# Two attention layers on one core: the third product bank behind the products with v, and the place of the quarter sums

## The chip, the core and the metric

The kernel runs on one core of one Trainium2 chip. The metric is the device time of one launch in microseconds (us), the median of three runs. The profile is of one further execution, recorded by the hardware profiler.

## What is computed

Two transformer layers in float32 over 4 images of 32 x 32 tokens and 768 channels, 12 heads of 64. Both normalise in groups, make q, k and v, add a relative-position bias to the scores, take the softmax, weigh v, project, and add the result to the input. The second also convolves q, k and v (3 x 3, per channel) and normalises them per head.

```python
# layer 0, of gn(x)
q, k, v = heads(x @ Wq + bq), heads(x @ Wk + bk), heads(x @ Wv + bv)
attn = q @ k.T / sqrt(64) + rel_bias_h[..., :, None] + rel_bias_w[..., None, :]
x = x + (softmax(attn) @ v) @ Wp + bp
# layer 1, of gn(x)
q, k, v = split(x @ w_qkv.T)
q, k, v = (layer_norm(dwconv3x3(t, w_pool)) for t in (q, k, v))
attn = q @ k.T * 64**-0.5 + rel_h[..., :, None] + rel_w[..., None, :]
x = x + (softmax(attn) @ v + q) @ w_proj.T + b_proj
```

## The kernel before

**Stages and pairs.** A stage is one image in one layer; the eight stages run in the order images 0 and 1 in layer 0, images 0 and 1 in layer 1, then images 2 and 3 likewise. A stage has six pairs of heads, so there are 48 pairs, counted from 0: pairs 0 to 5 are stage 0, pairs 12 to 23 and 36 to 47 belong to layer 1. While one pair is attended, the next is prepared. In layer 1 the preparation reaches further: a pair's first products are made half a pair earlier still.

**Steps.** `attend` (L663) goes through a pair in two halves of 512 queries (`c`), each in two batches of four key tiles (`g`). A batch makes four score tiles of 128 keys x 2 heads x 512 queries on TensorE (L724 q with k, L726 the bias), each followed by one exponential on ScalarE (L731) and one addition on VectorE into the running sum `acc` (L738, L740). Then come two steps of other work, behind the scores. Then follow the products with v (L746), and two more steps of other work, behind the products with v. A pair thus has 16 steps: 0, 1, 4, 5, 8, 9, 12, 13 lie behind scores and 2, 3, 6, 7, 10, 11, 14, 15 behind products with v. The sums over keys (z, L688) and the result's operations (L695 to L716) of a half are spread over the windows of the next half through the list `rest`.

**The order is written out by hand.** `plan` (L596) gives each pair's pieces with their steps, `at` (L787) files pieces under a step, and the loop at L827 issues them at that step in the order in which they were filed. Each engine works through its own instructions in that order. The pieces that matter here, with their steps in the pair before the one that they prepare:

- Layer 1: `padded(V, 0)` at 2, `centre(Q)` at 3 (two banks), `positions(0)` at 10, `positions(1)` at 11, `back(K, 0)` and `back(K, 1)` at 14, `split` at 12. Of the pair after that, `padded(Q, 1)` at 10 and `padded(K, 1)` at 14 (its steps -6 and -2).
- Layer 0: `sevens(Q, .)` at 0 and 2, `positions` at 6 and 8, `split` at 10. `sevens` uses a scheme of seven products of quarters in place of eight; its sums of quarters of the activations come from `mix_tokens` (L272), five additions on VectorE of 128 x 1536 elements (L280), two of them in place in `xn`, three into the shared buffer `quarters`.
- `split` (L577) rounds the bias on ScalarE (`high`, L582), subtracts it on VectorE (L583), and issues 16 DMAs on POOL (L593) that lay `high` and the rest, `whole`, out as the bias tiles.
- `group_norm` (L283) of the next stage in twelve pieces; its mean (`gn_mean`, L298, read on VectorE at L300) falls on step 14 of a stage's third pair.
- `project` (L758) of the stage before: twelve products in the first pair of a stage, each read on VectorE (L780). For image 0 in layer 1 a small product, `pbias` (L770), stands ahead of every second one.

**The banks of PSUM.** There are eight. `ps_a` has two, one pair of banks for the first and fourth score tile of a batch. `place_b` and `place_c` have two each, used as a pair by the second and the third score tile, and as single banks by the other work in between. One holds the products with v, and one, the sums' bank (`ps_small`), holds z, the small products of the group norm, `pbias`, and one of the products of `sevens`. Other work asks for a single bank through `bank` (L117), and `other_work` (L113) sets the order of places: behind scores b, b, c, c, behind products with v c, c, b, b, and round again. A tile that takes a place waits until the readers of what was there are done.

**The moved sums.** Where the stage before is of layer 0 too, `mix_tokens` stands on steps 72 to 76, counted from the first step of the stage before (L801); the pieces of that stage's last pair that read the quarters stand on 64 and 66, and the first piece that reads the new ones on 80. This happens for stages 1 and 5, so in pairs 4 and 28.

Of the kernel before, what the change touches and what calls it, by code (L numbers as in the profile page):

```python
# [45 lines left out]
def two_layers(ctx: ExitStack, tc: tile.TileContext, keep, x_in, wqkv, wproj, rels, windows, vrow, small, const, onehot, picks, out):  # L46
# [60 lines left out]

    place_b, place_c = Place("left"), Place("right")  # L110
    places = [place_b, place_c]

    def other_work(first, second):  # L113
        places[:] = [first, second]
        first.n = second.n = 0

    def bank(name):  # L117

        place = places[0]
        ps = place.single(name)  # L120
        if place.n % 2 == 0:
            places.reverse()
        return ps

    def small_bank(name):
        return ps_small.tile([P, 512], F32, tag="small", name=name)
# [20 lines left out]
    def col(c, lo=0, hi=P):  # L147
        return sm[lo:hi, c : c + 1]
# [15 lines left out]
    stages = [(b0 + k, layer) for b0 in range(0, B, 2) for layer in range(2) for k in range(2)]  # L164
# [38 lines left out]
    def shift(i):  # L203

        return 4 if i and items[i][1] == 0 and items[i - 1][1] == 1 else 0
# [3 lines left out]
    for i, (_, layer, hp) in enumerate(items):  # L209
        first = (i - 1) * 16 + shift(i)  # L210
# [8 lines left out]
    def load_xn(stage):  # L219
        b, layer = stage  # L220
        xn = xnp.tile([P, NC, T], F32, tag="xn", name="xn")
        src = rows(mid[b] if layer else x_in[b])
        for n in range(NC):
            nc.sync.dma_start(xn[:, n, :], src[:, n, :])
        xns[stage] = xn
# [46 lines left out]
    def mix_tokens(stage):  # L272


        x11, x12, x21, x22 = (xns[stage][:, n : n + 3, h : h + HALF] for n in (0, 3) for h in (0, HALF))
        for to, x, y, op in (
            (quarters[1], x11, x12, ALU.add), (x12, x12, x22, ALU.subtract), (quarters[2], x21, x22, ALU.add),
            (x21, x21, x11, ALU.subtract), (quarters[0], x11, x22, ALU.add),
        ):
            nc.vector.tensor_tensor(to, x, y, op)  # L280
            yield
# [57 lines left out]
    class Pair:  # L339
# [86 lines left out]
        def product(self, s, h):  # L426
            xn, w = xns[self.b, self.layer], weights[self.i, s]
            ps = bank("qkv")
            for n in range(NC):
                halves(ps, w[:, n, :], xn[:, n, h * HALF : (h + 1) * HALF], n == 0, n == NC - 1)  # L430
            if h:
                used((self.i, s))
            return ps
# [229 lines left out]
    def attend(pair, os):  # L663


        q, k, bias = pair.q, pair.k, pair.bias
        os.append(q)
        nonlocal found
        heads = [slice(j * D, (j + 1) * D) for j in range(2)]

        def more():
            nonlocal found
            if rest:
                found = rest.pop(0)(*found)

        for c in range(T // QC):
            cols = slice(c * QC, (c + 1) * QC)

            def copy(av):
                weighed = one.tile([P, QC], F32, tag="weighed", name="weighed")  # L680
                nc.scalar.copy(weighed, av)  # L681
                return weighed

            def sums(weighed, acc, c=c):

                z = small_bank("z")
                for j in range(2):
                    nc.tensor.matmul(  # L688
                        z[j * D : (j + 1) * D, :], cst[:, ONES : ONES + D], acc[:, j, :],
                        start=True, stop=True,  # L690
                    )
                at = 2 * (pair.i * (T // QC) + c)
                t = work.tile([P, QC], F32, tag="t", name="t", bufs=1)
                inv = work.tile([P, QC], F32, tag="inv", name="inv", bufs=1)
                nc.scalar.activation(t, z, AF.Copy, accum_out=seen[:, at : at + 1])  # L695

                nc.scalar.activation(inv, t, AF.Ln, bias=tiny)
                nc.scalar.activation(inv, inv, AF.Exp, scale=-1.0, accum_out=seen[:, at + 1 : at + 2])
                return weighed, t, inv

            def result(weighed, t, inv, cols=cols):

                nc.vector.scalar_tensor_tensor(t, t, -1.0, inv, ALU.mult, ALU.mult)
                nc.vector.scalar_tensor_tensor(inv, t, 2.0, inv, ALU.add, ALU.mult)

                if pair.layer:
                    nc.vector.tensor_tensor(inv, weighed, inv, ALU.mult)
                    nc.vector.scalar_tensor_tensor(q[:, cols], inv, col(LN + 4), q[:, cols], ALU.mult, ALU.add)
                else:
                    nc.vector.tensor_tensor(inv, weighed, inv, ALU.mult)  # L710
                return (inv,)

            def finish(inv, cols=cols):

                if not pair.layer:
                    nc.scalar.activation(q[:, cols], inv, AF.Identity, bias=col(pair.column(2)))  # L716

            for g in range(0, NKT, 4):
                es = []
                for kt, place in zip(range(g, g + 4), (None, place_b, place_c, None)):  # L720
                    keys = slice(kt * P, (kt + 1) * P)
                    ps = place.pair("s") if place else ps_a.tile([P, 2, 512], F32, tag="a", name="s")
                    for j, rows in enumerate(heads):
                        nc.tensor.matmul(ps[:, j, :], k[rows, keys], q[rows, cols], start=True, stop=False)  # L724
                    for j, rows in enumerate(heads):
                        nc.tensor.matmul(  # L726
                            ps[:, j, :], ones[rows, keys], bias[c][rows, kt // 2, :],
                            start=False, stop=True,
                        )
                    e = work.tile([P, 2, QC], F32, tag="e", name="e", bufs=4)  # L730
                    nc.scalar.activation(e, ps, AF.Exp)  # L731
                    es.append(e)
                other_work(place_b, place_c)
                more()
                if g == 0:
                    av = ps_av.tile([P, QC], F32, tag="av", name="av")
                    acc = work.tile([P, 2, QC], F32, tag="acc", name="acc", bufs=1)
                    nc.vector.tensor_tensor(acc, es[0], es[1], ALU.add)  # L738
                for e in es[2 * (g == 0) :]:
                    nc.vector.tensor_tensor(acc, acc, e, ALU.add)  # L740
                yield
                yield
                for t, e in enumerate(es):
                    kt = g + t
                    for j in range(2):
                        nc.tensor.matmul(  # L746
                            av[j * D : (j + 1) * D, :], pair.vt[:, kt, j * D : (j + 1) * D], e[:, j, :],
                            start=(kt == 0), stop=(kt == NKT - 1),
                        )
                other_work(place_c, place_b)  # L750
                more()
                if g + 4 == NKT:
                    rest.extend((sums, result, finish))
                    found = (copy(av), acc)
                yield
                yield
# [30 lines left out]
    def at(step, piece):  # L787
        events.setdefault(step, []).append(piece)

    n_steps = NKT * (T // QC)  # L790
    oss = [[] for _ in stages]
    for k in range(1, len(stages)):
        first = (k - 1) * NC * n_steps
        at(first + n_steps, lambda k=k: load_xn(stages[k]))
        norm = group_norm(stages[k])
        for r in range(12):
            at(first + 2 * n_steps + 2 + 3 * r, lambda norm=norm: next(norm, None))
        if stages[k][1] == 0:
            mix = mix_tokens(stages[k])
            for r in range(5):  # L800
                at(first + 5 * n_steps + (r // 3 if stages[k - 1][1] else r - 8), lambda mix=mix: next(mix, None))  # L801
        elif stages[k - 1][1] == 0:
            at(first + 4 * n_steps + 6, lambda: [nc.gpsimd.memset(pad, 0.0) for pad in pads])
    mix = mix_tokens(stages[0])
# [11 lines left out]
    for k, stage in enumerate(stages):  # L816
        steps = project(stage, oss[k])
        first = (k + 1) * NC * n_steps
# [7 lines left out]
    step = 0  # L826
    for i, pair in enumerate(pairs):  # L827
        for _ in attend(pair, oss[i // NC]):
            for piece in events.pop(step, ()):
                piece()  # L830
            step += 1
# [311 lines left out]
```

## Time and profile before

| what | us |
|---|---|
| median of three runs (3982.46 to 3984.02) | 3983.66 |
| the profiled execution | 3979.48 |
| its span | 3977.6 |
| TensorE busy | 3898.5 |
| VectorE busy | 2492.3 |
| ScalarE busy | 1840.8 |
| POOL busy | 411.5 |

PE is TensorE's matmul side, PEld its weight loads, DVE VectorE, ACT ScalarE, POOL GpSimd. A line of the timeline has the start and the duration in us, engine, line and operation, then what is written and read (out<-in), how many instructions were merged into it, and in brackets the idle time before it with what ended it. A line of the waits has the waiting instruction, what it waited for, the time in us, how often, and the longest. Idle time of TensorE is what counts, as it is the fullest engine. Its matmuls are pipelined and their ends are modelled, so the distance from one start to the next is the measure.

### The profile page before, as it was taken

The page shows a single profiled execution, that of the slowest core. Times are in us where ns is not written, and L with a number is a line of the kernel's source. Part 1 is how long each engine was busy: PE and PEld are TensorE (multiplying, and loading weights), DVE is VectorE, ACT ScalarE, POOL GpSimd, SP SyncE. Part 2 cuts the span into 40 slices and gives each one's busy share as a digit, 9 for nine tenths or more (in the row PEclk, how much of TensorE's full clock was granted, in tenths as well). Part 3 has the DMA queues.
Part 4 walks back from the last instruction along what each step waited for, and adds up shares of the span by engine and source line. Part 5 has one row for each costly group of instructions (what it writes and reads, how often), then busy time and mean ns, then how long its engine had stood idle before and what let it go on. Part 6 is the DMA issues. An engine that isn't in the chain of part 4 may idle for free.

```text
span 3977.6 us, 79975 instructions
## 1 busy us (share of the span) xinstructions
PE 3898.5 (98%) x35026; PEld 1736.9 (44%) x35026; DVE 2492.3 (63%) x2794; ACT 1840.8 (46%) x2717; POOL 411.5 (10%) x776
## 2 busy tenths in 40 slices
PE   7999999999999999999899999999999999999999
PEld 3535434534344444444444445355443444434443
DVE  2455524557489984799633554245675898848883
ACT  2454424555355552455433544254542555425552
POOL 0111100110000100000011010001100011000010
PEclk9999999999999999999999999999999999999999
DMA  5343242221411312212133222423124121131122
GB/s 161 85 117 115 72 135 74 65 55 50 131 44 34 91 38 86 63 41 70 42 110 89 54 72 64 147 58 76 43 59 124 38 50 47 44 104 42 38 47 76
DMA packets 179044, 293.33 MB, mean 74 GB/s; under 512 B 22528, under 2 KB 77952, under 8 KB 178688
## 3 DMA queue, kind: packets, MB, share of 16 engines
q1 hardware_dynamic: 117248, 187.41, 15.1%
q0 software_dynamic: 61440, 100.71, 11.0%
q8 instruction: 279, 4.57, 0.5%
q14 instruction: 77, 0.63, 0.0%
HBM read 153.36 MB, written 34.01 MB: 47 GB/s over the span
## 4 chain that ended last, share of the span: by engine, by line
PE 90%; DVE 6%; DMA 2%; issue 1%; ACT 1%; POOL 0%; DVEq 0%; SPq 0%; ACTq 0%
PE qkv L131 19%; PE s L724 15%; PE av L746 15%; PE proj L131 13%; PE m3m L131 4%; PE m4m L131 4%; PE s L726 4%; PE m1m L131 4%; PE ln_c L131 3%; PE rel L566 3%; PE z L688 2%; PE m L131 2%; DVE shared L508 2%; DVE acc L740 2%; PE ln_t L544 1%
## 5 line engine op out<-in xcount | busy, mean ns | idle before, releaser
L731 ACT ACTIVATE e<-s 128x1024 f32<-128x1024 f32 x768 | 780.7, 1025 | 470.6 <-PE s L726 437.4
L724 PE MATMUL s<-q,k 64*128 64x512 f32 x3072 | 817.3, 608 | 11.1 <-ACT whole L572 7.6
L740 DVE TENSOR_TENSOR acc<-acc,e 128x1024 f32<-128x1024 f32 x576 | 705.6, 1225 | 184.9 <-ACT e L731 135.5
L131 PE MATMUL qkv<-xn,wqkv_t 128*64 128x512 f32 x3648 | 815.7, 596 | 2.9 <-DVE xn L314 2.9
L508 DVE SCALAR_TENSOR_TENSOR shared<-shared,sm 128x1056 f32<-128x1056 f32 x576 | 758.4, 1317 | 14.9
L726 PE MATMUL s<-bias,ones 64*128 64x512 f32 x1536 | 613.6, 792 | 14.5 <-DMA bias<-whole 9.6
L746 PE MATMUL av<-e,vt 128*64 128x512 f32 x2624 | 594.2, 594 | 0.0
L593 POOL DMA_DIRECT2D bias<-high x384 | 204.0, 549 | 3295.5 <-ACT high L582 3047.3
L131 PE MATMUL proj<-q,wproj_t 128*64 128x512 f32 x2304 | 504.2, 593 | 0.0
L131 PEld LDWEIGHTS qkv<-xn,wqkv_t 128*64 128x64 f32 x3648 | 253.8, 137 | 487.5 <-issue 482.2
L491 ACT ACTIVATE shared<-qkv,sm 128x512 f32<-128x512 f32 (+1 forms) x288 | 129.3, 502 | 591.2 <-PE qkv L131 591.2
L724 PEld LDWEIGHTS s<-q,k 64*128 64x128 f32 x3072 | 277.7, 187 | 281.1 <-issue 203.9
L746 PEld LDWEIGHTS av<-e,vt 128*64 128x64 f32 x2624 | 185.2, 137 | 346.7 <-issue 319.2
L738 DVE TENSOR_TENSOR acc<-e 128x1024 f32<-128x1024 f32 x96 | 117.5, 1224 | 305.0 <-ACT e L731 293.8
L131 PEld LDWEIGHTS proj<-q,wproj_t 128*64 128x64 f32 x2304 | 163.2, 137 | 316.4 <-issue 315.9
L726 PEld LDWEIGHTS s<-bias,ones 64*128 64x128 f32 x1536 | 150.0, 188 | 202.8 <-issue 194.7
L593 POOL DMA_DIRECT2D bias<-whole x384 | 206.0, 563 | 121.5 <-DVE whole L583 112.0
L681 ACT COPY weighed<-av 128x512 f32<-128x512 f32 x96 | 56.4, 587 | 301.7 <-PE av L746 301.7
L780 DVE SCALAR_TENSOR_TENSOR x<-proj,sm,x 128x512 f32<-128x512 f32 x48 | 36.1, 751 | 217.4 <-PE proj L131 213.1
L780 DVE SCALAR_TENSOR_TENSOR x<-proj,pbias,x 128x512 f32<-128x512 f32 x48 | 36.0, 750 | 216.1 <-PE proj L131 211.7
L131 PEld LDWEIGHTS ln_c<-cst,shared 128*64 128x64 f32 x2304 | 131.7, 138 | 48.9 <-issue 41.4
L131 PE MATMUL ln_c<-cst,shared 128*64 128x128 f32 x2304 | 139.7, 275 | 6.9 <-DVE shared L508 6.2
(121 smaller groups left out, 3744.8 us busy)
## 6 DMA issues: line engine op xcount, KB each, us to landing
bias<-high POOLq DMA_DIRECT2D x384, 128.0 KB, 2.8
bias<-whole POOLq DMA_DIRECT2D x384, 128.0 KB, 3.0
wqkv_t<-in_wqkv SPq DMA_DIRECT2D x78, 384.0 KB, 3.1
wqkv_t<-mixed SPq DMA_DIRECT2D x66, 384.0 KB, 3.1
wproj_t<-in_wproj SPq DMA_DIRECT2D x48, 384.0 KB, 3.8
wqkv_t<-in_wqkv SPq DMA_DIRECT2D x66, 192.0 KB, 2.5
xn<-in_x SPq DMA_DIRECT2D x24, 512.0 KB, 7.6
x<-in_x SPq DMA_DIRECT2D x48, 256.0 KB, 2.8
```

What stands on the lines that cost most here:

```text
L131: nc.tensor.matmul(ps[lo : lo + D], a[:, lo : lo + D], b, start=start, stop=stop, **kw)
L491: nc.scalar.activation(self.pad[s][:, rows, there : there + src.shape[2]], src, AF.Identity, bias=col(self.column(s)))
L508: nc.vector.scalar_tensor_tensor(y, window, tap, y, ALU.mult, ALU.add)
L566: nc.tensor.matmul(ps[lo : lo + S, k * S : (k + 1) * S].rearrange("p (b c) -> p b c", b=2), rel[rows, 2 * self.layer + i, first : first + ...
L593: nc.gpsimd.dma_start(sets, some.unsqueeze(1).to_broadcast([D // 2, 2, QC]))
L688: nc.tensor.matmul(z[j * D : (j + 1) * D, :], cst[:, ONES : ONES + D], acc[:, j, :], start=True, stop=True,)
L724: nc.tensor.matmul(ps[:, j, :], k[rows, keys], q[rows, cols], start=True, stop=False)
L726: nc.tensor.matmul(ps[:, j, :], ones[rows, keys], bias[c][rows, kt // 2, :], start=False, stop=True,)
L731: nc.scalar.activation(e, ps, AF.Exp)
L738: nc.vector.tensor_tensor(acc, es[0], es[1], ALU.add)
L740: nc.vector.tensor_tensor(acc, acc, e, ALU.add)
L746: nc.tensor.matmul(av[j * D : (j + 1) * D, :], pair.vt[:, kt, j * D : (j + 1) * D], e[:, j, :], start=(kt == 0), stop=(kt == NKT - 1),)
```

## The change

Behind the products with v, the third request for a single bank in a window gets the sums' bank (`small_bank`) instead of a bank of place_b; the order there becomes c, c, sums' bank, b, b. Behind scores it stays b, b, c, c. And where a stage of layer 0 follows one of layer 0, the five quarter sums of `mix_tokens` are issued on steps 68, 68, 69, 69, 70 instead of 72 to 76.

```diff
     place_b, place_c = Place("left"), Place("right")
-    places = [place_b, place_c]
-
-    def other_work(first, second):
-        places[:] = [first, second]
-        first.n = second.n = 0
+    behind_scores, behind_av = (place_b, place_b, place_c, place_c), (place_c, place_c, None, place_b, place_b)
+    turn = list(behind_av)
+
+    def other_work(places):
+        turn[:] = places
+        place_b.n = place_c.n = 0
 
     def bank(name):
 
-        place = places[0]
-        ps = place.single(name)
-        if place.n % 2 == 0:
-            places.reverse()
-        return ps
+        place = turn.pop(0)
+        turn.append(place)
+        return place.single(name) if place else small_bank(name)
...
-                other_work(place_b, place_c)
+                other_work(behind_scores)
                 more()
...
-                other_work(place_c, place_b)
+                other_work(behind_av)
                 more()
...
             mix = mix_tokens(stages[k])
             for r in range(5):
-                at(first + 5 * n_steps + (r // 3 if stages[k - 1][1] else r - 8), lambda mix=mix: next(mix, None))
+                step = 5 * n_steps + r // 3 if stages[k - 1][1] else 4 * n_steps + 4 + r // 2
+                at(first + step, lambda mix=mix: next(mix, None))
```

## Prediction

> **What bounds the kernel now.** I read the busy times first, then the waits of TensorE, then the timeline around each wait that the change can touch.
>
> ```profile
> PE 3898.5 (98%) x35026; PEld 1736.9 (44%) x35026; DVE 2492.3 (63%) x2794; ACT 1840.8 (46%) x2717; POOL 411.5 (10%) x776
> ```
>
> TensorE is busy for 98% of the span and its clock is full after the start. No matmul is removed, so only its stalls can be won. The list of waits names those of the score tiles:
>
> ```profile
> PE s L726 <- DMA bias<-whole: 9.6, 5, 2.4
> PE s L724 <- ACT whole L572: 7.6, 18, 0.4
> ...
> PEld s L724 <- ACT whole L572: 19.4, 20, 1.1
> PEld s L724 <- ACT shared L522: 14.9, 24, 0.6
> ```
>
> (Columns: us in total, times, longest.) The ends of matmuls are modelled, so I price stalls by starts. An undisturbed batch of scores behind the products with v starts its tiles 1.20 and then 1.09 us apart (pair 13, keys 4 to 7 of the first half):
>
> ```profile
> 1116.72 1.13 PE L724 MATMUL s<-q,k 64*128 64x512 f32 x4
> ...
> 1117.92 1.02 PE L724 MATMUL s<-q,k 64*128 64x512 f32 x4
> ```
>
> In the same pair, where `positions(1)` had the third bank, the second tile starts 1.78 us after the first, and only once ScalarE has copied that bank:
>
> ```profile
> 1141.53 1.13 PE L724 MATMUL s<-q,k 64*128 64x512 f32 x4
> ...
> 1143.31 1.13 PE L724 MATMUL s<-q,k 64*128 64x512 f32 x4 [0.41 <-ACT whole L572]
> ...
> 1144.50 1.02 PE L724 MATMUL s<-q,k 64*128 64x512 f32 x4
> ```
>
> Where the second half of `centre(Q)` had it, the second tile starts 1.35 us after the first, 0.06 us after L522 ends:
>
> ```profile
> 1103.17 1.13 PE L724 MATMUL s<-q,k 64*128 64x512 f32 x4
> ...
> 1104.52 1.13 PE L724 MATMUL s<-q,k 64*128 64x512 f32 x4
> ...
> 1103.86 0.60 ACT L522 COPY shared<-ln_c 128x512 f32<-128x512 f32 x1
> ```
>
> The other stall lies at the start of pairs 5 and 29. The first scores are there, their bias is not: `split`'s subtraction (L583) stands on VectorE behind quarter sums (L280), and POOL issues the bias DMAs only after it.
>
> ```profile
> 398.40 1.75 DVE L280 TENSOR_TENSOR shared<-xn 128x1536 f32<-128x1536 f32 x1
> 400.06 1.22 DVE L583 TENSOR_TENSOR whole<-whole,high 128x1024 f32<-128x1024 f32 x1
> ...
> 401.57 2.08 POOL L593 DMA_DIRECT2D bias<-whole  x4 [5.36 <-DVE whole L583]
> ...
> 405.30 0.50 PE L726 MATMUL s<-bias,ones 64*128 64x512 f32 x2 [2.32 <-DMA bias<-whole]
> ```
>
> **What the Trainium skill says.** "Perfetto Trace Analysis", Optimization Strategy: the same gap repeated on the engine that should be full can mean that PSUM is short for the next tile. The trace agrees: 1.35 us stands in all 24 pairs during which layer 1 is prepared. The same page, Tensor Engine Instruction: matmul ends are estimates; hence starts here. "TensorE: Matmul & The Clock Gate", What's actually happening: a TensorE idle for a window of some 3.4 us falls to half clock. After the stall of pair 29 two tiles start 2.13 us apart instead of 1.09, the half clock; here 2.34 us of idle were enough, and the measurement decides.
>
> **Part 1, the third bank.** Placing the pieces of `plan` and `project` on their steps gives 74 windows behind products with v that ask for three banks or more; 66 have three, four have four, four have six. Most belong to layer 1's preparation, three a pair: `padded(V,0)` and both halves of `centre(Q)` (steps 2, 3); `positions(0)`, the next pair's `padded(Q,1)`, `positions(1)` (steps 10, 11); `back(K)` twice and the next `padded(K,1)` (step 14). Until now the third took place_b, which the second score tile needs.
>
> - Steps 10, 11: the distances are 1.78 + 1.19 against 1.20 + 1.09, so 0.69 us (0.72 in the pairs after a mean of the group norm). Of 24 pairs, 18 show it; pairs 12, 18, 36, 42 (with projections behind) don't, nor pairs 22 and 46, which have no next pair of layer 1. Three of the 18 (14, 20, 38) I set aside below: 12 x 0.69 + 3 x 0.72 = 10.4 us.
> - Steps 2, 3: 1.35 + 1.19 against 1.20 + 1.09, so 0.26 us in each of 24. Pairs 14, 20, 38 lose it again at a VectorE-bound tile (step 8), pairs 22 and 46 in their latency-bound ends: 19 x 0.26 = 5.0 us.
> - Step 14: ScalarE reads `padded(K,1)` from 1163.69 to 1164.59, the second tile starts at 1164.78, 1.20 after the first. Nothing to win.
> - Windows of projection: VectorE empties each product within 0.9 us of its end, and their next scores are undisturbed. I cost them at nothing; the cover is that VectorE has caught up there.
>
> The sums' bank gets new tenants, so three queues must be looked at. `centre(Q)`'s half starts 8 us after the sums (z, L688) have been read at 1093.64. The sums of the next pair start at 1168.13, 3.5 us after `padded(K,1)` was read. `positions(1)` is read by 1143.25, `padded(K,1)` starts at 1158.28. All free. One is not: in pairs 14, 20 and 38 `gn_mean` stands in that bank just ahead of `padded(K,1)`, and its reader is VectorE, late by its taps:
>
> ```profile
> 1236.45 1.51 PE L131 MATMUL qkv<-xn,wqkv_t 128*64 128x512 f32 x6
> ...
> 1236.97 0.15 DVE L300 COPY gmean<-gn_mean 128x1 f32<-128x1 f32 x1
> ```
>
> VectorE has a single idle stretch between 1163 and 1240, so its clock is fixed there: the product will start at 1237.12 + 0.06 instead of 1236.45. That costs 3 x 0.73 = 2.2 us and also swallows those pairs' gain, left out above. Behind that waiting product stand on TensorE the next pair's scores; VectorE and ScalarE wait for those.
>
> In pair 18 one projection's bias (`pbias`) follows a projection in the sums' bank. VectorE reads that at 1560.53, the bias starts at 1560.88: free by 0.35 us. A product that waits for two engines may carry one more semaphore instruction, 51 ns by the row of L724; over 66 windows this is 0 to 3.4 us, and could as well fall away elsewhere. I take 0.
>
> **Part 2, the quarter sums.** Ten VectorE instructions move (five a stage, stages 1 and 5; 1.75 us each), no DMA, nothing on SP or POOL. They leave steps 72 to 76 for 68 to 70. Two before the result's operations and one ahead of L583 fall away from its front. In the new place VectorE is done with its sums of exponentials at 381.7 and idle until 389.08 (7.4 us); five at a pitch of about 1.7 take 8.5, to 390.2. The next sums of exponentials start 1.1 us late, end at 394.0, the result's three take to 396.1, L583 runs 396.1 to 397.3, against 401.2 now. POOL follows by 0.4 us and the bias lands 3.7 us after that issue (401.57 to 405.30): 401.4, needed at 402.41. The margin is 1.0 us, so the stall goes whole. Its size by starts: pair 5 2.56 us; pair 29 2.84 and, at the low clock, 1.05 and 0.24 more: 6.7 us in all. Bounds 0 and 6.7, as the old stall can do no more than vanish. The quarters' earlier readers end at 374, the norm at step 64: no new wait. The scores become next to wait only for q and k.
>
> **Sum.** -10.4 - 5.0 + 2.2 - 6.7 = -19.9 us. The profiled execution took 3979.48 (span 3977.6 and 1.9 around it); it becomes 3959.6. The median of the three runs lies 4.2 above it, so I forecast **3963.8 us**, 0.50% less. A change under 0.2%, 8 us, can't be told from none.
>
> **Rivals.**
>
> 1. *Slower: the sums' bank becomes the queue.* If ScalarE read `padded(K,1)` only behind the four exponentials of the next scores, at 1169.27, the sums would start 1.2 us late in each of 24 pairs: +28.8, net +8.9, 3992.6 us. It decides once that read ends after 1168.13. Against it: ScalarE reads 0.1 us after the product ends, ahead of the exponentials, and is busy for 44 of 77 us. Chance 0.06.
> 2. *VectorE takes over in layer 1.* It is busy 66.8 of 77 us in an ordinary pair and 72.9 in one with group norm. If it paces all pairs, part 1 brings nothing beside its +2.2, part 2 its 6.7: about 3979. For: the pairs with group norm. Against: ordinary pairs gain only 0.95 us of 9 idle. Chance 0.09.
> 3. *Part 2 misses* because the margin of 1.0 us is eaten (VectorE's late start, POOL): -13.2, 3970.5. Chance 0.10.
> 4. *The change doesn't do it*: the allocator's waits keep the score tile behind another tile of place_b, and the sums still delay L583. 3983.7. Chance 0.03.
>
> **Numbers.** My forecast has 0.72, with its own range 3957 to 3970: from 3.4 us of semaphores and a gain of group-norm pairs halved, to 3 us for the pairs that I set aside and 4 for the spread of medians. Cases of 0.72 and 0.10 are faster: 0.82. Cases 2 and 4 are the same: 0.12. Case 1 is slower: 0.06. The range 3957 to 3973 leaves out cases 1, 2, 4, about 0.18.
>
> **What would show it.** In the profile after, ACT whole and ACT shared vanish as releasers of L724; score tiles of pair 13 stand 1.20 and 1.09 apart in all batches, and an ordinary pair takes 75.3 instead of 76.3 us. `qkv` waits three times for DVE gmean, 0.7 to 1.7 us each. The bias waits of L726 fall from five to three, L280 ends before L583 in pair 4. I am wrong in part 1 if z or ln_c waits in TensorE's list rise by what L724's fall, in part 2 if L726 at the start of pair 5 still waits.

## The result and the profile after

The changed kernel takes **3959.69 us** (median of five runs, 3957.07 to 3963.90) against 3982.46 us before (five runs, 3980.34 to 3984.02). The ratio is 0.9945, with a 95% interval from 0.9930 to 0.9959. The profiled execution has a span of 3957.8 us, 19.8 less than before; the forecast was 19.9 less.

First the busy times, then the waits of TensorE in the changed kernel, as the list of waits has them (us in total, times, longest):

```profile
PE 3884.8 (98%) x35026; PEld 1743.2 (44%) x35026; DVE 2492.4 (63%) x2794; ACT 1835.7 (46%) x2717; POOL 411.4 (10%) x776
```

```profile
PE s L726 <- DMA bias<-high: 7.1, 2, 4.2
...
PE qkv L131 <- DVE gmean L300: 4.1, 3, 1.4
...
PE s L724 <- ACT e L731: 3.5, 3, 1.2
...
PE s L726 <- DMA bias<-whole: 2.9, 3, 2.4
...
PEld s L724 <- ACT whole L572: 2.1, 9, 0.2
```

The same instructions ran, as the unchanged counts show, and only stalls went. TensorE's busy time fell by 13.7 us with the same matmuls, so part of the stalls had been counted as busy. ScalarE's copy of `whole` (L572) no longer releases a matmul of the score tiles and is left with 2.1 us before their weight loads; L522 is gone from both. The waits for `bias<-whole` fell from five to three. One new row matters: `qkv` waits three times for VectorE's copy of the group norm's mean. Another, 0.2 us at the very end, is a projection behind the last small product, as the projections there draw from the sums' bank too.

The timeline shows the batch of scores in pair 13 that had waited for `positions(1)`, and ScalarE's copies beside it:

```profile
1137.76 1.13 PE L724 MATMUL s<-q,k 64*128 64x512 f32 x4
...
1138.95 1.02 PE L724 MATMUL s<-q,k 64*128 64x512 f32 x4
...
1138.46 1.01 ACT L572 COPY whole<-rel 64x512 f32<-64x512 f32 x1
```

The second tile starts 1.19 us after the first, while L572 is still reading the third bank (to 1139.47). TensorE no longer waits for that copy. The batch behind `centre(Q)` in the same pair reads alike, 1099.66 and 1100.85.

At the start of pair 5 the bias is now there:

```profile
388.92 1.75 DVE L280 TENSOR_TENSOR shared<-xn 128x1536 f32<-128x1536 f32 x1
390.59 1.22 DVE L738 TENSOR_TENSOR acc<-e 128x1024 f32<-128x1024 f32 x1
...
396.44 1.22 DVE L583 TENSOR_TENSOR whole<-whole,high 128x1024 f32<-128x1024 f32 x1
...
397.95 2.08 POOL L593 DMA_DIRECT2D bias<-whole  x4 [1.38 <-DVE whole L583]
...
402.22 1.13 PE L724 MATMUL s<-q,k 64*128 64x512 f32 x4
402.78 0.80 PE L726 MATMUL s<-bias,ones 64*128 64x512 f32 x2
```

The last quarter sum stands ahead of the sums of exponentials (L738), no quarter sum stands between those and L583 any more, and the bias product starts 0.56 us after the first scores, the undisturbed distance.

The new wait stands in pair 14:

```profile
1232.50 0.15 DVE L300 COPY gmean<-gn_mean 128x1 f32<-128x1 f32 x1
...
1232.71 2.37 PE L131 MATMUL qkv<-xn,wqkv_t 128*64 128x512 f32 x10 [1.36 <-DVE gmean L300]
```

`padded(K,1)` starts 0.06 us after VectorE has read the mean, and TensorE idled 1.36 us for it.

For the rest I use the length of a pair, from the start of its first score tile to that of the next pair's. It separates what the change does from what varies from one execution to the next. Two kernels were profiled twice, the changed one and that of experiment 3: between their two executions pairs 0 to 4 together differ by 0.9 and 2.2 us, pairs 23 and 24 and the two ends of a run by 0.2 to 1.4 us each; the 24 pairs in which layer 1 is prepared (11 to 22 and 35 to 46), pair 46 apart, by less than 0.05.

| us | before | changed | bank alone | sums alone | last window as before |
|---|---|---|---|---|---|
| an ordinary pair (13) | 76.31 | 75.35 | 75.35 | 76.31 | 75.35 |
| a pair with projections (12) | 137.56 | 137.30 | 137.30 | 137.57 | 137.30 |
| a pair with the mean (14) | 78.17 | 78.90 | 78.90 | 78.17 | 77.46 |
| pair 5 | 75.89 | 73.27 | 75.85 | 73.27 | 73.23 |
| pair 29 | 77.74 | 73.27 | 77.67 | 73.87 | 73.37 |
| all 24 pairs preparing layer 1 | 2066.4 | 2052.6 | 2052.6 | 2066.4 | 2048.3 |

### The profile page after: what moved, and what is told of

Read it like the earlier page. It is cut to its first block, busy times and chain, and to the rows that moved or that the text cites. A ratio compares the mean times of both kernels' runs of the same rounds, so it can differ in the third digit from the quotient of the medians.

```text
span 3957.8 us, 79930 instructions
## 1 busy us (share of the span) xinstructions
PE 3884.8 (98%) x35026; PEld 1743.2 (44%) x35026; DVE 2492.4 (63%) x2794; ACT 1835.7 (46%) x2717; POOL 411.4 (10%) x776
## 4 chain that ended last, share of the span: by engine, by line
PE 88%; DVE 9%; DMA 1%; issue 1%; ACT 0%; POOL 0%; DVEq 0%; SPq 0%; ACTq 0%
PE qkv L131 18%; PE s L724 16%; PE av L746 15%; PE proj L131 13%; PE m3m L131 4%; PE s L726 4%; PE m1m L131 4%; PE m4m L131 4%; DVE shared L508 3%; PE rel L566 3%; PE ln_c L131 3%; PE z L688 2%; DVE acc L740 2%; PE m L131 2%; PE ln_t L544 1%
## 5 line engine op out<-in xcount | busy, mean ns | idle before, releaser
L738 DVE TENSOR_TENSOR acc<-e 128x1024 f32<-128x1024 f32 x96 | 117.5, 1224 | 293.7 <-ACT e L731 282.4
```

## The experiments

**1. The bank alone.** The changed kernel with the old place of the quarter sums:

```diff
-                step = 5 * n_steps + r // 3 if stages[k - 1][1] else 4 * n_steps + 4 + r // 2
-                at(first + step, lambda mix=mix: next(mix, None))
+                at(first + 5 * n_steps + (r // 3 if stages[k - 1][1] else r - 8), lambda mix=mix: next(mix, None))
```

> The third bank behind the products with v is the sums' bank, the quarter sums stay on steps 72 to 76. My theory (two separate stalls that add up): span 3977.6 - 15.7 (pairs 11, 13, 16 ... 0.95 us shorter each, pairs 12, 18, 36, 42 and 22, 46 0.26) + 2.2 (pairs 14, 20, 38, 0.73 longer each) = about 3964; pairs 5 and 29 keep their 75.9 and 77.7 us and their wait for the bias. Rival (the quarter sums' late end also paced the bank): the gain falls short of 13 us.

Measured: 3966.77 us, ratio 0.9962 (0.9949 to 0.9976). The 24 pairs shorten by 13.8 us in all, each by the amount expected. Its span, 3967.1, is 3 us over what was expected: pairs 23 and 24 took 1.3 us more, the end after the last pair's first scores 2.3 us more. The banks that the edit moves there don't explain it: the changed kernel has the same ones, and took 0.2 us less and 0.3 us more there than the kernel before. The waits keep the bias and lose the copies:

```profile
PE s L726 <- DMA bias<-whole: 9.5, 5, 2.4
...
PE qkv L131 <- DVE gmean L300: 4.1, 3, 1.4
```

**2. The quarter sums alone.** The kernel before with this edit:

```diff
-                at(first + 5 * n_steps + (r // 3 if stages[k - 1][1] else r - 8), lambda mix=mix: next(mix, None))
+                step = 5 * n_steps + r // 3 if stages[k - 1][1] else 4 * n_steps + 4 + r // 2
+                at(first + step, lambda mix=mix: next(mix, None))
```

> The quarter sums are issued on steps 68 to 70, the banks are as before. My theory: pairs 5 and 29 lose their wait for the bias, 2.6 and 4.1 to 4.5 us, and nothing else moves: span about 3970.7, and with the bank alone the two gains add up to the whole change. Rival (the stall goes elsewhere: the sums of exponentials of pair 4 start 1.1 us late and hold something up): pair 4 becomes longer by about 1 us, and the gain is 5 us or less.

Measured: 3973.82 us, ratio 0.9980 (0.9971 to 0.9988). Pairs 5 and 29 shorten by 2.62 and 3.87 us; pair 4, where the sums now stand, lengthens by 0.17 and not by the rival's 1 us. Pair 29's gain lies under the 4.1 to 4.5 expected because of a later product (below, under the mis-sized terms). The span of 3975.9 hides most of that: in that execution the first scores came 1.3 us later, pairs 23 and 24 took 1.5 us more and the end after the last pair's first scores 1.8. Its waits are the mirror image:

```profile
PE s L724 <- ACT whole L572: 7.5, 18, 0.4
...
PE s L726 <- DMA bias<-whole: 3.7, 3, 2.0
```

Timed on one chip against the same runs of the kernel before (3981.28), the bank takes 14.5 us, the sums 7.5, both together 21.6. The two stalls are separate, and they add up (22.0 against 21.6).

**3. The last window as before.** The changed kernel, but on steps 14 and 15 the third bank is one of place_b:

```diff
-                other_work(behind_av)
+                other_work(behind_av if (c, g) != (1, 4) else (place_c, place_c, place_b, place_b))
```

> The whole change, but in the window on steps 14 and 15 the third bank is one of place_b as before. My theory (padded(K,1) of pairs 14, 20 and 38 waits in the sums' bank for VectorE's late read of the group norm's mean, and the third bank of this window never held up a score tile): pairs 14, 20, 38 take about 77.5 us instead of 78.9, the qkv waits for DVE gmean vanish, ordinary pairs stay at 75.35: 4.3 us less than the whole change, span about 3953.5. Rival (those pairs are paced by VectorE anyway): the 1.4 us come back as another wait on VectorE in pairs 14, 20, 38 or 15, 21, 39, and the span stays at 3957.8. Second rival (the window needs the sums' bank): the second score tile of steps 0 and 1 stands more than 1.20 us after the first in 24 pairs.

Measured: 3953.70 us, ratio 0.9934 (0.9920 to 0.9947); in a second set of runs, expected at 3952 to 3956, 3953.15, ratio 0.9932 (0.9918 to 0.9946). Pairs 14, 20 and 38 take 77.46 us, 1.44 less than in the changed kernel, and of the other 21 none moves by more than 0.02. The second score tile of steps 0 and 1 stands 1.19 or 1.20 us after the first in all 24 pairs, so this window had no need of the sums' bank. The waits of TensorE from 1155 to 1240 us, which hold pair 14, no longer name the mean:

```profile
PE s L724 <- ACT e L731: 1.2, 1, 1.2
PE ln_c L131 <- DVE t_ln L157: 0.2, 1, 0.2
```

Both rivals fall: the 1.44 us came from the bank, not from VectorE's pace. By pairs that is 4.3 us, as expected; the medians lie 6.0 apart.

**4. The changed kernel again, beside these.** No edit.

> The changed kernel once more, beside the parts: about 3958 span and 20 to 23 us less than before.

Measured: 3959.65 us, ratio 0.9948 (0.9935 to 0.9962). The 24 pairs have the same lengths to within 0.05 us.

**5. All five quarter sums ahead of the split.**

```diff
-                step = 5 * n_steps + r // 3 if stages[k - 1][1] else 4 * n_steps + 4 + r // 2
+                step = 5 * n_steps + r // 3 if stages[k - 1][1] else 4 * n_steps + 8 + r // 2
```

> The whole change, but the quarter sums on steps 72, 72, 73, 73, 74: all five ahead of the split's subtraction instead of three (before) or none (changed). My theory (each sum ahead of L583 puts the bias 1.7 us later, and TensorE waits for it): L583 ends about 3.4 us later than before, pairs 5 and 29 take about 75.9 + 3.4 = 79.3 and 77.7 + 3.4 = 81.1 us instead of 73.3. Rival (the wait came from POOL's issue or from the DMAs, not from VectorE's queue): pairs 5 and 29 stay near 75.9 and 77.7 us.

Measured in one run: pair 5 takes 82.07 us, pair 29 81.06.

```profile
400.47 1.75 DVE L280 TENSOR_TENSOR shared<-xn 128x1536 f32<-128x1536 f32 x1
402.14 1.22 DVE L583 TENSOR_TENSOR whole<-whole,high 128x1024 f32<-128x1024 f32 x1
...
400.46 1.13 PE L724 MATMUL s<-q,k 64*128 64x512 f32 x4
407.43 0.80 PE L726 MATMUL s<-bias,ones 64*128 64x512 f32 x2 [5.83 <-DMA bias<-whole]
407.99 1.94 PE L724 MATMUL s<-q,k 64*128 64x512 f32 x4
```

From the first scores to the bias product it is 6.97 us instead of 3.45, 3.5 more for two more sums ahead of L583 at 1.7 us each. The wait follows VectorE's queue, sum by sum, and the rival (POOL or the DMAs set it) falls. Pair 5 lost 2.7 us more than that, as TensorE came back at half clock: the four matmuls at 407.99 take 1.94 us instead of 1.02, and the clock granted from 406.23 to 413.06 is 0.50.

**6. The sums' bank on steps 10 and 11 alone.**

```diff
-                other_work(behind_av)
+                other_work(behind_av if (c, g) == (1, 0) else (place_c, place_c, place_b, place_b))
```

> The whole change, but only the window on steps 10 and 11 gives its third bank to the sums' bank; elsewhere it is one of place_b. My theory (the terms add up per window): ordinary pairs 76.3 - 0.69 = 75.6 us, pairs 14, 20, 38 about 77.5 us, the second score tile of steps 4 and 5 stands 1.35 us after the first again in 24 pairs, span about 5 us above that of the run with only the last window as before, 3957. Rival (one of the two windows carries all of the gain): ordinary pairs at 75.35 or at 76.3.

Measured in one run: ordinary pairs take 75.61 us, pairs 14, 20 and 38 77.46, and behind `centre(Q)` the old distance of 1.35 us is back in all 24:

```profile
1097.00 1.13 PE L724 MATMUL s<-q,k 64*128 64x512 f32 x4
...
1098.35 1.13 PE L724 MATMUL s<-q,k 64*128 64x512 f32 x4
```

So the window on steps 10 and 11 is worth 0.70 us a pair, that on steps 2 and 3 0.26. In pair 14 the second is worth nothing: 77.46 with it and without it.

**7 and 8. The group norm sooner.** Experiment 3 with the next stage's norm begun 7 or 8 steps sooner in layer 1 (10 in the place of 11 in the second):

```diff
-            at(first + 2 * n_steps + 2 + 3 * r, lambda norm=norm: next(norm, None))
+            at(first + (n_steps + 11 if stages[k - 1][1] else 2 * n_steps + 2) + 3 * r, lambda norm=norm: next(norm, None))
```

> The run with the last window as before, and in layer 1 the group norm of the next stage starts 7 steps sooner (steps 27, 30, ... instead of 34, 37, ...), so that two of its three pieces of statistics lie in the pair before and its mean and variance in windows where the sums' bank has no third product. My theory (pairs 14, 20, 38 are paced by VectorE, 74 of 78 us busy before, and 5.4 us of that move to pairs with 8 us to spare): pairs 14, 20, 38 take 75.4 to 76 us instead of 77.5, pairs 13, 19, 37 75.4 to 76.3 instead of 75.35; span 3946 to 3951. Rival (the wait only moves along with the statistics): pairs 13, 19, 37 take 77 us or more and the span stays at 3952.

> As the run with the norm earlier, but one step sooner still (26, 29, ...): the mean then lies on step 6, two steps ahead of the sums z that use its bank, instead of one. My theory (what is left in pairs 14, 20, 38 is z waiting for VectorE's read of the mean): z no longer waits for DVE gmean, those pairs take 75.4 to 75.9 us instead of 76.6, span 1 to 4 us below 3949.5. Rival (VectorE's queue still paces them): 76.4 us or more, with another wait on VectorE in its place.

Measured with 11: 3952.23 us, ratio 0.9931 (0.9917 to 0.9944); pairs 14, 20 and 38 take 76.63 us, above the 75.4 to 76 expected, pairs 13, 19 and 37 stay at 75.35. What I had overlooked is in the waits from 1100 to 1300 us: the mean on step 7 is the tenant just ahead of z on step 8.

```profile
PE z L688 <- DVE gmean L300: 0.4, 1, 0.4
PE ln_c L131 <- DVE t_ln L157: 0.2, 1, 0.2
```

With 10 the first of these rows is gone, and the list has no wait of TensorE's matmuls in pair 14. But pairs 14, 20 and 38 take 76.03 us, above the 75.4 to 75.9 expected, and pairs 15, 21 and 39 0.35 to 0.70 more than in experiment 3. Measured: 3953.13 us, ratio 0.9929 (0.9915 to 0.9943), beside 3953.15 for experiment 3 on the same chip; the span of 3951.8 isn't below that with 11 either. By pairs the norm sooner is worth about 2.9 us (3 x 1.43 less 1.41 in pairs 15, 21, 39); in the timed medians that does not show. Of the wait for the mean the theory held. That those pairs would come down to 75.4 left out TensorE's own work: both small products of the norm now lie in pair 14, and each puts what follows it 0.32 us later:

```profile
1185.95 0.38 PE L298 MATMUL gn_mean<-mv,cst 128*128 128x1 f32 x2
1186.27 1.13 PE L724 MATMUL s<-q,k 64*128 64x512 f32 x4
...
1215.69 0.38 PE L307 MATMUL gn_var<-gd,cst 128*128 128x1 f32 x2
1216.01 0.65 PE L131 MATMUL qkv<-xn,wqkv_t 128*64 128x512 f32 x2
```

75.35 + 2 x 0.32 is 75.99. The pairs after them grew although `gn_var` had left them; that VectorE's work moved there is likely (`ln_c` waits 0.2 us for it in pair 15), but was not tested.

Experiment 3 beats both kernels by one line: on one chip its five runs took 3953.45 to 3955.75 us, those of the changed kernel 3957.38 to 3963.00.

## Why the prediction was right

**Where the time went.** By pairs, the bank gave 13.8 us (2066.4 to 2052.6) where the sum had 15.4 - 2.2 = 13.2, and the quarter sums gave 2.62 + 4.47 = 7.1 where it had 6.7. Together that is 20.9; the span fell by 19.8, as pairs 3 and 27 took 1.4 us more, without a part of the change in them. That the span met the forecast's 19.9 to 0.1 us is luck: the parts are out by 0.6 and 0.4, and what else varies between executions is larger. The timed medians fell by 22.8 and, beside the parts, by 21.6; single runs of the changed kernel spread by 7 us.

**Term by term.** Steps 10 and 11: 0.69 us forecast, 0.70 by experiment 6. Steps 2 and 3: 0.26 forecast and measured. Step 14: nothing to win, shown by experiment 3. Windows of projection: pairs 12, 18, 36 and 42 gained the 0.26 of `centre(Q)` and nothing else; VectorE kept up there, as the forecast said. The extra semaphore instruction, costed at 0, does not show: in the 24 pairs all batches stand at 1.19 or 1.20 and then at 1.08 or 1.09 us.

**The gn_mean wait.** 0.73 us a pair were forecast from VectorE's fixed clock, and pairs 14, 20 and 38 lengthened by 0.72 to 0.73. VectorE ended the mean's copy 73.54 us after pair 14's first scores, before and after. The step also said that VectorE "swallows" those pairs' gain. Experiments 3 and 6 take that apart: with the bank freed, 0.71 of the 0.72 us of steps 10 and 11 comes through, so it was the bank that withheld it. The 0.26 of steps 2 and 3 is lost at the fourth tile on step 8, as forecast: 2.14 us after the third before, it stands 2.40 after it now. It waits for ScalarE's first exponential, which stands behind L153, which waited for VectorE (L527). Before, then changed:

```profile
1197.44 1.13 PE L724 MATMUL s<-q,k 64*128 64x512 f32 x4 [0.89 <-ACT e L731]
...
1192.98 1.13 PE L724 MATMUL s<-q,k 64*128 64x512 f32 x4 [1.15 <-ACT e L731]
```

**Terms that were mis-sized.** Pairs 22 and 46 were forecast to lose their 0.26 in their latency-bound ends, and kept 0.25 to 0.27. Pair 29 gained 4.47 and not 4.13, but its first batch gave 4.11 of that (8.67 to 4.56 us from its first scores to z); the rest lies at a later product, m4m, which is 3.07 us long before, 2.68 after and 3.30 in experiment 2, so it isn't the change's. Without it part 2 gave the 6.7 us forecast. Both are below what a timed run can tell.

**Part 2.** L583 was forecast at 396.1 and L738 at 390.2; they stand at 396.44 and 390.59 in an execution whose pair 5 begins 0.37 us later. The margin of 1.0 us was enough, so the third rival did not come about. The second rival, VectorE as the pace of layer 1, holds for three pairs only, at that fourth tile and at `ln_c` behind it (0.2 us each). The first, a queue in the sums' bank, happened only where a VectorE read stood in it, as priced. That z would wait did not come about until experiment 7 put the mean ahead of it.

## What to carry to other kernels

When other work borrows a bank that the next main batch needs, price the loan by the distance between that batch's starts, not by the idle time in the list of waits, and lend a bank whose next tenant comes late. Before lending it, list every tenant in program order with the engine that empties it: a reader on a late engine turns the free bank into a stall, and it is enough to spare that one window. When a stall ends on a DMA, look for what stands ahead of the instruction that feeds the DMA in its engine's queue; moving work into that engine's idle stretch cost 0.17 us here.

## What the runs showed of the hardware that was not expected

A stall of the same length can cost TensorE half its clock or not. After 2.3 us of idle in pair 29 of the kernel before two tiles stood 2.13 us apart; after 2.3 us in pair 5 of the same execution 1.09:

```profile
2373.73 0.80 PE L726 MATMUL s<-bias,ones 64*128 64x512 f32 x2 [2.34 <-DMA bias<-whole]
2374.29 1.94 PE L724 MATMUL s<-q,k 64*128 64x512 f32 x4
...
2376.43 1.26 PE L724 MATMUL s<-q,k 64*128 64x512 f32 x4
```

With the longer wait of experiment 5 both fell to half clock, and pair 5 paid 2.7 us beyond the wait itself.

The traces also hold the clock that TensorE was granted, and the eleven of them together show what the fall goes by. (It was not full all the time after the start, as the prediction has it.) In each execution the stretches at half clock start whole multiples of 3.413 us apart: in the kernel before at 62.6, 233.3, 322.1, 1895.6, 1912.7, 1933.2, 2373.5 and 3861.7 us, and once more at the end. They last 3.41, 6.83 or 10.24 us, unless the program ends first.

Each execution can thus be cut into windows on its own grid, and TensorE's idle time in each added up, with the ends of matmuls as modelled. Of the windows at full clock, 79 have 2.03 us or more of it, and half clock followed every one. Some 12,460 have less than 1.59 us, and it followed none; of the 29 between it followed 12. Pair 29's stall put 2.1 us into one window, 2370.1 to 2373.5; pair 5's was cut by the border at 404.0 into 1.0 and 1.3 us. What pair 29 lost to the clock hung on where its stall fell on the grid. Pair 3 shows the same: it takes 78.8 to 79.7 us in the seven executions with such a stretch in it, 76.5 to 77.2 in the four without.

For ScalarE's copy of `whole` the list of waits gave the matmuls 7.6 us and the weight loads 19.4; by the starts it was about 0.7 us in each of 18 pairs, 12.6 in all. Neither row is the price.
